# Moving a 2 MB weight load and two of its sums into the first pair of groups, and seeding a fourth output tile from the bias

## The chip, the cores and the metric

The kernel runs on one core of a Trainium2 chip. A core has five engines that run their own instruction queues side by side: PE (matrix products), DVE (vector), ACT (scalar and activations), POOL (GpSimd) and SP (here used to issue transfers). They meet only through semaphores. PE writes to PSUM, which is divided into banks; the other data lie in SBUF. Transfers between HBM and SBUF run on 16 DMA engines that all the queues share. The metric is the device time in microseconds (us); before the change it is 458.37 us, the median of three runs (458.12 to 458.46).

## What is computed

The input x has 32 sequences of 128 rows of 512 numbers. A conditioning vector per sequence gives a shift, a scale and a gate, once for each of two halves. In the reference, cut to what matters:

```
norm = layernorm(x) * (1 + scale) + shift;  norm = where(m, norm, 0)
ssm_out = where(m, mlp(norm, ssm) + mlp(norm, bwd), 0)
x = x + gate_msa * ssm_out                      # first half, masked rows only
ff_norm = layernorm(x) * (1 + scale_mlp) + shift_mlp
h = gelu(ff_norm @ ff_w1 + ff_b1)               # 512 -> 1024
return x + gate_mlp * (h @ ff_w2 + ff_b2)       # 1024 -> 512
```

`mlp(u, w)` is `gelu(u @ w1 + b1) @ w2 + b2`. All is float32.

## The kernel before

**First half.** Only the masked rows need it. They are gathered into four tiles of 128 rows, called slots. Their hidden layer is `hidden`, their second product is `project`. The output bias of the first half, `b2` (the sum of ssm_b2 and bwd_b2), is for tiles 0, 1 and 2 copied by ACT into a PSUM bank ahead of the products (`seeded_with_bias`, L236); the products then add to it. Tile 3 has no seed: its product goes into a bank of another pool, and DVE adds `b2` afterwards in `finish_late`, as the first of its three steps (L1367, L1369, L1370). The finished rows go to a buffer in HBM, `x1_rows`, from which POOL later gathers them back over the x tiles (`take_first_half`, L864). A row of `b2` is also kept in HBM (`b2_row`, L1346), for a loop at the end of the kernel that runs only where the masked rows fill more than the four tiles.

**Second half.** The 32 sequences are done in four pairs of two groups (four sequences to a group). Both products, `ff_w1` and `ff_w2` (here `fw1` and `fw2`), are done by a scheme with seven block products in place of eight, on two levels for the first. It needs differences of weight blocks. For `fw1`, DVE makes them in the opening; four of the larger ones (`weight_sums`) are stored to HBM (`t_rows`) and read back by `load_weights` into the two tiles `tw` when a stream needs them. For `fw2` there are four differences, `fw2_of.combine(0)` to `combine(3)` (line L387, 128x1024 numbers each): 0 gives t3, 1 replaces b12 of `fw2` in place, 2 gives t2 and 3 gives t4. Before the change 0 and 1 are made at the end of the opening, 2 and 3 inside the first pair's second product, which starts with the raw block b11, and then takes b12.

**FirstProduct** runs seven streams in the order 1, 2, 5, 6, 3, 7, 4. A stream has seven phases P1 to P7, of four matmuls each. From the third stream on a window weaves a new stream with the one before it: new P5, new P1, old P3, old P7, new P2, new P6, old P4 (positions 0 to 6). Window 2 starts stream 5, window 3 stream 6, window 4 stream 3, window 5 stream 7, window 6 stream 4. Streams 5 and 7 use one `tw` tile, 6 and 4 the other, so the third load waits for the last matmul of stream 5 and the fourth for that of stream 6. Between the phases stand:

- after P6 a DVE sum (L1121) that must be done before the same stream's P3;
- after P1 a seed, by DVE (L1140) or ACT (L1142), which must be done before P2;
- after P5 an ACT copy of the bank to SBUF (`p_m`, L1110), and additions on POOL (`with_p5`, L1147; `after`, L1176; `late_sum`, L1180), on which later L1121 and L1140 depend;
- ACT's copies and activations of the finished blocks (L1154, L1058).

The dictionary `fills` says what else is issued at a position: `put(3, 6, f)` issues f in window 3 after position 6.

**Order.** Nothing is scheduled by a planner in this part: every engine runs its instructions in the order in which the code issues them. On SP a transfer that has to wait holds everything behind it. In the opening SP issues, in this order: the transposing loads of xT, the 2 MB of `fw2` (`load_behind_gathers`, behind a one-element POOL memset), three stores of weight sums to `t_rows`, two stores to `x1_rows`, `b2_row`, `fb2`, two loads of the next pair's x, the last two stores to `x1_rows`, the first `tw` load, two more loads of x, the second `tw` load. PSUM tiles come from three pools that hand out their banks in turn; a new tile waits for the last reader of the bank it gets.

Of the kernel before, what the change touches and what calls it, by code (L numbers as in the profile page):

```python
# [14 lines left out]
ALU = mybir.AluOpType  # L15
# [7 lines left out]
def kernel(  # L23
# [49 lines left out]
    nc = tc.nc  # L73
# [23 lines left out]
    ps_h = ctx.enter_context(tc.tile_pool(name="ps_h", bufs=3, space=bass.MemoryType.PSUM))  # L97
# [16 lines left out]
    def broadcast_rows(t, vec, queue):  # L114

        n = vec.shape[0] // D
        each = t.shape[0] // n
        for j in range(n):
            queue.dma_start(
                t[j * each : (j + 1) * each, :],  # L120
                vec[ts(j, D)].rearrange("(o d) -> o d", o=1).to_broadcast([each, D]),
            )
# [12 lines left out]
    def load_blocks(t, w):  # L135
        nc.sync.dma_start(t, w.rearrange("(k p) f -> p k f", p=P))

    def load_behind_gathers(t, w):
        nc.gpsimd.memset(t[0:1, 0, 0:1], 0.0)
        load_blocks(t, w)  # L140
# [7 lines left out]
    w2 = ssm.tile([P, HC, D], F32, name="w2")  # L148
# [20 lines left out]
    def own_statistics(t, n, name):  # L169

        for i in range(n):
            st = stp.tile([P, 6], F32, tag="st", name=f"st_{name}_{i}")
            row = t[:, i]
            nc.vector.bn_stats(st, row[:, :D])
            nc.vector.bn_aggr(row[:, D : D + 2], st)
        var = t[:, :, D + 1]
        nc.vector.tensor_scalar(var, var, EPS, None, ALU.add)
        nc.gpsimd.tensor_tensor(var, var, half[:, :n], ALU.pow)

    def group_of_tiles(name):  # L180
        return xnp.tile([P, G, D], F32, tag="xn", name=f"xn_{name}")
# [19 lines left out]
    def hidden(xT, n, w, bcol, func, name, pool, parts=range(HC), after=None):  # L201

        h = []
        for f in parts:
            ph = ps_h.tile([P, 512], F32, tag="h", name=f"ph_{name}_{f}")
            for k in range(KC):
                nc.tensor.matmul(  # L207
                    ph[:, :n], w[:, k, ts(f, P)], xT[:, k, :], start=(k == 0), stop=(k == KC - 1)
                )
            t = pool.tile([P, n], F32, tag="h", name=f"h_{name}_{f}", bufs=HC)  # L210
            nc.scalar.activation(t, ph[:, :n], func, bias=biasT[:, bcol + f : bcol + f + 1])
            h.append(t)
            for g in (after or {}).get(f, ()):
                g()
        return h

    def project(i, h, w, name, between=None, bank=(ps_o, "o"), seeded=None):

        pool, tag = bank
        po = seeded or pool.tile([P, 512], F32, tag=tag, name=f"po_{name}_{i}")  # L220
        for f in range(HC):
            if between and f in between:
                between[f]()
            nc.tensor.matmul(  # L224
                po,
                h[f][:, ts(i, P)],
                w[:, f, :],
                start=(f == 0 and seeded is None),
                stop=(f == HC - 1),
                skip_group_check=seeded is not None,  # L230
            )
        return po

    def seeded_with_bias(at):
        po = ps_o.tile([P, 512], F32, tag="o", name=f"po_s{at}")
        nc.scalar.copy(po, b2)  # L236
        return po

    def gated(po, bias, gate, name):

        t = tp.tile([P, D], F32, tag="t", name=f"t_{name}")
        nc.vector.tensor_tensor(t, po, bias, ALU.add)
        nc.vector.tensor_tensor(t, t, gate, ALU.mult)
        return t
# [117 lines left out]
    def finish_slots(at, po, gate):  # L362
        t = tp.tile([P, 1, D + 2], F32, tag="t", name=f"t_s_{at}")
        row = t[:, 0, :D]
        nc.vector.tensor_tensor(row, po, gate, ALU.mult)
        nc.vector.tensor_tensor(row, row, xc[at], ALU.add)
        own_statistics(t, 1, f"s_{at}_x1")
        nc.sync.dma_start(x1_wide[ts(at, P), :], t[:, 0])
        return lambda: nc.sync.dma_start(x1_rows[ts(at, P), :], row)
# [20 lines left out]
    def load_side(p, side, spare=()):  # L390

        tiles = []
        for c in range(2):
            b = (2 * p + side) * G + 2 * c
            t = spare[c] if c < len(spare) else x_tile(b)
            nc.sync.dma_start(t, x[b : b + 2].rearrange("b s d -> s b d"))
            tiles.append(t)
        return tiles
# [184 lines left out]
    b2 = ssm.tile([P, D], F32, name="b2")  # L583
# [51 lines left out]
    fw2 = fwp.tile([P, HC, D], F32, name="fw2")  # L635
# [57 lines left out]
    def in_blocks(t):  # L693
        return t.rearrange("p g (h f) -> p (g h) f", f=2 * P)
# [22 lines left out]
    def store_weight_sums(*which, queue=nc.sync):  # L717
        for j in which:
            queue.dma_start(t_rows[j - 1, :, 4:], t_sum[j][1][:, :3])
            queue.dma_start(t_rows[j - 1, :, :4], t_sum[j][0])  # L720
# [30 lines left out]
    h1 = []  # L751
    for f in range(KC):
        hidden_of_tile(f, 1)
        for done in (f - 1, f) if f % 2 else ():
            t = ssm.tile([P, NH], F32, tag="h", name=f"h_s0_{done}", bufs=HC)
# [19 lines left out]
    po_s = [seeded_with_bias(0)]  # L775
# [4 lines left out]
    own_statistics(raw[2], 2, "x_2")  # L780
    b2_row = dram.tile([1, D], F32, name="b2_row")
    store_rows = [finish_slots(0, project(0, h1, w2, "s0", seeded=po_s[0]), gs[0])]
    own_statistics(raw[3], 2, "x_3")
    t = in_blocks(group_of_tiles("tw_3"))
    t_sum[3] = [t[:, :4], t[:, 4:]]
# [65 lines left out]
    of_x = {}  # L851
# [6 lines left out]
    fw2_of = Weights(fw2, HC // 2, D // 2, t_2)  # L858
# [69 lines left out]
    def turned(xn, xT, queues, which=range(4)):  # L928

        R = 32  # L930
        src = xn.rearrange("p k i (q c) -> p q k i c", c=R)
        dst = xT.rearrange("p k (i b c) -> p b k i c", b=P // R, c=R)
        for b in which:
            for q in range(P // R):
                queues[(b + q // 2) % len(queues)].dma_start(dst[ts(q, R), b], src[ts(b, R), q])  # L935
# [403 lines left out]
    def turn(k):  # L1339
        return lambda: transposed(1, xn_b, xT[1], k)  # L1340

    def turn_rows(b):
        return lambda: turned(xn, xT[0], (nc.sync, nc.scalar), (b,))

    def load_of_pair_1():
        nc.sync.dma_start(b2_row, b2[0:1, :])  # L1346
        broadcast_rows(fb2, ff_b2, nc.sync)
        x_of[1] = [load_side(1, 0, spare), None]

# [3 lines left out]
        3: [turn_rows(0), lambda: weight_sums(4)],  # L1353
        4: [turn_rows(1)],
        5: [turn_rows(2)],
        6: [turn_rows(3), lambda: load_behind_gathers(fw2, ff_w2), lambda: store_weight_sums(4, 1, 2)] + store_rows,
        7: [load_of_pair_1],
    }
    h1 = hidden(xT_t, NH, w1, 0, AF.Gelu, "s1", ssm, after=after)
# [1 line left out]
    for k in range(KC):  # L1361
        scaled(0, xT[0], k)

    def finish_late(at, po, bias=None):
        t = tp.tile([P, D], F32, tag="t", name=f"t_s_{at}")
        if bias is not None:
            nc.vector.tensor_tensor(t, po, bias, ALU.add)  # L1367
            po = t
        nc.vector.tensor_tensor(t, po, gs[at], ALU.mult)  # L1369
        nc.vector.tensor_tensor(t, t, xc[at], ALU.add)  # L1370
        nc.sync.dma_start(x1_rows[ts(at, P), :], t)

    finish_late(2, project(0, h1, w2, "s2", {2 * k: turn(k) for k in range(KC)}, seeded=po_s[2]))
    po = project(1, h1, w2, "s3", bank=(ps_h, "h"))
    of_x[0] = TokenBlocks(0, xT)
    for j in (1, 2):
        of_x[0].one(j)
    fw2_of.combine(0, 1)
    for j in (3, 4):
        of_x[0].one(j)  # L1380
    finish_late(3, po, b2)
    first_half.close()
    hp = straight.enter_context(tc.tile_pool(name="hp", bufs=1))
    gp = straight.enter_context(tc.tile_pool(name="gp", bufs=1))
# [25 lines left out]
    for p in range(NP):  # L1410
# [4 lines left out]
        def put(w, n, f, *args):  # L1415
            fills.setdefault(w, {}).setdefault(n, []).append(lambda: f(*args))
# [7 lines left out]
        for n, at in enumerate(((2, 4), (2, 4), (2, 6), (2, 6) if more_pairs else (3, 1))):  # L1424
            put(*at, now.token_sums, 4, n)
        put(3, 6, now.load_weights, 3)
        put(4, 6, now.load_weights, 4)
        second = SecondProduct(p, now.h, xs)
        if p == 0:
# [127 lines left out]
    with tc.If(more > 0):  # L1557
        b2 = lp.tile([P, D], F32, name="b2_l")
# [10 lines left out]
        with tc.For_i(0, more, 1):  # L1569
# [12 lines left out]
            for half_no, (mod, was, wbs, bias, bcol, func) in enumerate(  # L1582
# [25 lines left out]
                t = gated(project(0, h_l, wb, f"l{half_no}"), bias, gate_l, f"l{half_no}")  # L1608
# [59 lines left out]
```

## Time and profile before

The profiled execution took 457.94 us, of which the span of its instructions is 456.2 us. Over the span PE is busy 445.3 us (98%), DVE 332.8 (73%), ACT 176.9 (39%) and POOL 161.2 (35%). The granted clock of PE is 0.999 of full speed.

The table gives busy microseconds of each engine in stretches of the span, and the mean busy share of the 16 DMA engines. The opening ends, and the first pair's streams begin, at 84.45 us; the first pair's second product begins at 127.6, the second pair at 171.6.

| stretch, us | PE | DVE | ACT | POOL | DMA share |
|---|---|---|---|---|---|
| 60 to 70 | 10.00 | 8.58 | 2.37 | 6.02 | 0.63 |
| 70 to 80 | 10.00 | 7.56 | 7.53 | 0.00 | 0.97 |
| 80 to 90 | 9.80 | 9.70 | 2.50 | 0.00 | 1.00 |
| 90 to 100 | 7.26 | 8.05 | 3.59 | 6.45 | 1.02 |
| 100 to 110 | 10.00 | 8.77 | 5.19 | 8.45 | 0.15 |
| 110 to 130 | 20.00 | 14.04 | 10.42 | 16.25 | 0.27 |
| 130 to 150 | 20.00 | 18.83 | 7.47 | 5.76 | 0.58 |
| 150 to 180 | 30.00 | 20.96 | 14.28 | 0.00 | 0.49 |

A row is read against its length: PE is short of the stretch's length only where it waited. An engine can be far from full over a stretch and still be late for one instruction, so the waits of single instructions have to be read too. Where one line of the profile names what ended an idle time, it is the last of the awaited events.

### The profile page before, as it was taken

The page shows a single profiled execution, that of the slowest core. Times are in us where ns is not written, and L with a number is a line of the kernel's source. Part 1 is how long each engine was busy: PE and PEld are TensorE (multiplying, and loading weights), DVE is VectorE, ACT ScalarE, POOL GpSimd, SP SyncE. Part 2 cuts the span into 40 slices and gives each one's busy share as a digit, 9 for nine tenths or more (in the row PEclk, how much of TensorE's full clock was granted, in tenths as well). Part 3 has the DMA queues.
Part 4 walks back from the last instruction along what each step waited for, and adds up shares of the span by engine and source line. Part 5 has one row for each costly group of instructions (what it writes and reads, how often), then busy time and mean ns, then how long its engine had stood idle before and what let it go on. Part 6 is the DMA issues. An engine that isn't in the chain of part 4 may idle for free.

```text
span 456.2 us, 6196 instructions
## 1 busy us (share of the span) xinstructions
PE 445.3 (98%) x2161; PEld 370.9 (81%) x2161; DVE 332.8 (73%) x570; ACT 176.9 (39%) x387; POOL 161.2 (35%) x155
## 2 busy tenths in 40 slices
PE   8999999979999999999999999999999999999995
PEld 4784485668888888888888888888888888888884
DVE  4797887978779749895796398867963995534645
ACT  3123126244543551545435515454355154552000
POOL 4230560079770000697700006977000027560000
PEclk9999999999999999999999999999999999999999
DMA  7999549982208725822187258221772442222022
GB/s 233 382 352 403 232 70 261 339 343 96 80 22 221 115 60 203 290 96 82 34 214 106 64 198 293 94 84 43 201 111 62 152 149 82 80 92 94 0 93 96
DMA packets 83201, 70.98 MB, mean 156 GB/s; under 512 B 63292, under 2 KB 64268, under 8 KB 82142
## 3 DMA queue, kind: packets, MB, share of 16 engines
q1 hardware_dynamic: 67994, 58.41, 41.0%
q0 software_dynamic: 4400, 10.74, 7.0%
q10 hardware_dynamic: 10772, 1.39, 2.2%
q8 instruction: 19, 0.31, 0.3%
q14 instruction: 16, 0.13, 0.1%
HBM read 56.84 MB, written 13.70 MB: 155 GB/s over the span
## 4 chain that ended last, share of the span: by engine, by line
PE 80%; DMA 13%; DVE 4%; SPq 1%; issue 1%; POOL 0%; ACT 0%; POOLq 0%; ACTq 0%; DVEq 0%
PE a_o L1283 23%; PE a_m L1096 20%; PE e_o L1283 18%; PE e_m L1096 15%; DMA fw<-in_L_cond_ff_w_dram 7%; DMA tw<-t_rows 2%; DMA w<-in_L_cond_ssm_w_dram 1%; PE ph_s L207 1%; DVE t L387 1%; DMA xT<-xn 1%; DMA x_wide<-t_s 1%; PE last L1283 1%; SPq L935 1%; DMA x<-x_wide,slot_i 1%; DVE fw L387 0%
## 5 line engine op out<-in xcount | busy, mean ns | idle before, releaser
L1147 POOL TENSOR_TENSOR ha<-p_m,ha 128x512 f32<-128x512 f32 x20 | 25.8, 1289 | 176.8 <-ACT ha L1154 167.4
L1283 PE MATMUL e_o<-fw,ha 128*128 128x256 f32 x256 | 57.9, 379 | 0.0
L918 ACT ACTIVATE xT<-xT,modT 128x128 f32<-128x128 f32 x112 | 44.0, 480 | 33.0 <-DMA xT<-xn 32.1
L1283 PE MATMUL a_o<-t,hb 128*128 128x256 f32 x240 | 54.1, 379 | 0.0
L1283 PEld LDWEIGHTS e_o<-fw,ha 128*128 128x128 f32 x256 | 48.7, 190 | 6.5
L1283 PEld LDWEIGHTS a_o<-t,hb 128*128 128x128 f32 x240 | 45.7, 190 | 6.1
L1058 ACT ACTIVATE hb<-hb,biasT 128x256 f32<-128x256 f32 x64 | 29.0, 500 | 27.9 <-POOL hb L1180 19.4
L1110 ACT COPY p_m<-e_m 128x512 f32<-128x512 f32 x27 | 15.8, 585 | 50.1 <-PE e_m L1096 50.1
L864 POOL DMA_INDIRECT x<-x_rows,slot_i x24 | 28.5, 1186 | 6.8 <-issue 4.9
L224 PE MATMUL po_s<-w,h_s 128*128 128x512 f32 x64 | 28.7, 596 | 0.9 <-DMA w<-in_L_cond_bwd_w_dram 0.9
L1147 POOL TENSOR_TENSOR hb<-p_m,hb 128x512 f32<-128x512 f32 x20 | 29.4, 1470 | 0.3
L1283 PE MATMUL a_o<-t,s 128*128 128x256 f32 x128 | 28.9, 380 | 0.0
L1283 PE MATMUL a_o<-fw,ha 128*128 128x256 f32 x128 | 28.9, 379 | 0.0
L1283 PE MATMUL e_o<-fw,s 128*128 128x256 f32 x128 | 28.9, 379 | 0.0
L1154 ACT COPY ha<-e_m 128x512 f32<-128x512 f32 x32 | 18.5, 579 | 25.2 <-PE e_m L1096 24.7
L1283 PEld LDWEIGHTS a_o<-t,s 128*128 128x128 f32 x128 | 24.4, 190 | 3.2
L1283 PEld LDWEIGHTS a_o<-fw,ha 128*128 128x128 f32 x128 | 24.4, 190 | 3.3
L1283 PEld LDWEIGHTS e_o<-fw,s 128*128 128x128 f32 x128 | 24.4, 190 | 3.2
L1121 DVE TENSOR_TENSOR e_m<-a_m,ha 128x512 f32<-128x512 f32 x20 | 13.9, 697 | 16.7 <-POOL ha L1147 6.6
L1058 ACT ACTIVATE ha<-e_m,biasT 128x256 f32<-128x256 f32 x48 | 20.0, 467 | 14.7 <-PE e_m L1096 12.5
L1096 PE MATMUL a_m<-xT,tw 128*128 128x256 f32 x96 | 24.7, 380 | 0.0
L1126 DVE TENSOR_TENSOR hb<-a_m,hb 128x512 f32<-128x512 f32 x20 | 13.7, 685 | 15.0 <-PE a_m L1096 15.0
(235 smaller groups left out, 904.5 us busy)
## 6 DMA issues: line engine op xcount, KB each, us to landing
tw<-t_rows SPq DMA_DIRECT2D x16, 896.0 KB, 5.5
x<-in_x_dram SPq DMA_DIRECT2D x16, 512.0 KB, 12.0
gate<-gate_rows POOLq DMA_DIRECT2D x8, 1024.0 KB, 5.2
out_dram<-x SPq DMA_DIRECT2D x15, 512.0 KB, 4.4
xT<-xn SPq DMA_DIRECT2D x92, 64.0 KB, 2.4
fw<-in_L_cond_ff_w_dram SPq DMA_DIRECT2D x2, 2048.0 KB
ada_f<-in_L_cond_ffada_w_dram SPq DMA_DIRECT2D x4, 768.0 KB, 13.9
ada_a<-in_L_cond_ada_w_dram SPq DMA_DIRECT2D x4, 512.0 KB, 5.3
```

The lines of the kernel that those rows point to most:

```text
L207: nc.tensor.matmul(ph[:, :n], w[:, k, ts(f, P)], xT[:, k, :], start=(k == 0), stop=(k == KC - 1))
L224: nc.tensor.matmul(po, h[f][:, ts(i, P)], w[:, f, :], start=(f == 0 and seeded is None), stop=(f == HC - 1), skip_group_check=seeded is no ...
L864: nc.gpsimd.indirect_dma_start(out=xs[i // G][i % G // 2][:, i % 2], out_offset=None, in_=x1_rows, in_offset=bass.IndirectOffsetOnAxis(ap= ...
L918: nc.scalar.activation(out, src, AF.Identity, bias=shift, scale=scale)
L1058: nc.scalar.activation(dst[:, n], src[:, n], AF.Gelu_apprx_tanh, bias=biasT[:, f : f + 1])
L1096: nc.tensor.matmul(bank[:, ts(n, QT)], self.w_block(j, product)[:, ts(n, P)], self.x_block(j, product), start=(product in ("P1", "P5") and ...
L1110: nc.scalar.copy(p5, e)
L1121: nc.vector.tensor_tensor(e, a, p5, add)
L1126: nc.vector.tensor_tensor(dst, a, dst if prior else self.p5[j], add)
L1147: nc.gpsimd.tensor_tensor(self.place(RESULT[j], c), self.p5[j], other, ALU.add)
L1154: nc.scalar.copy(self.place(RESULT[j], c), src)
L1283: nc.tensor.matmul(part, src[:, k, ts(i, P)], w[product][:, k, :], start=(last and k == 0), stop=True, skip_group_check=True,)
```

## The change

It does three things.

1. `b2_row` is stored right after the first tile's rows, ahead of the third weight sums, and no longer ahead of the load of `fb2`.
2. A fourth bank is seeded with `b2` as soon as the first tile's bank has been read. Tile 3's product adds to it, and `finish_late` has two DVE steps instead of three.
3. The load of `fw2` leaves the opening, and the memset ahead of it goes. It is issued in the first pair at the end of window 3, between the third and the fourth `tw` load; `combine(0)` moves to the end of window 5 and `combine(1)` to position 3 of window 6. `combine(2)` and `combine(3)` stay.

```diff
     store_rows = [finish_slots(0, project(0, h1, w2, "s0", seeded=po_s[0]), gs[0])]
+    nc.sync.dma_start(b2_row, b2[0:1, :])
+    po_s.append(seeded_with_bias(3))
     own_statistics(raw[3], 2, "x_3")
...
     def load_of_pair_1():
-        nc.sync.dma_start(b2_row, b2[0:1, :])
         broadcast_rows(fb2, ff_b2, nc.sync)
...
-        6: [turn_rows(3), lambda: load_behind_gathers(fw2, ff_w2), lambda: store_weight_sums(4, 1, 2)] + store_rows,
+        6: [turn_rows(3), lambda: store_weight_sums(4, 1, 2)] + store_rows,
...
-    def finish_late(at, po, bias=None):
+    def finish_late(at, po):
         t = tp.tile([P, D], F32, tag="t", name=f"t_s_{at}")
-        if bias is not None:
-            nc.vector.tensor_tensor(t, po, bias, ALU.add)
-            po = t
         nc.vector.tensor_tensor(t, po, gs[at], ALU.mult)
...
-    po = project(1, h1, w2, "s3", bank=(ps_h, "h"))
+    po = project(1, h1, w2, "s3", seeded=po_s[3])
     of_x[0] = TokenBlocks(0, xT)
-    for j in (1, 2):
+    for j in range(1, 5):
         of_x[0].one(j)
-    fw2_of.combine(0, 1)
-    for j in (3, 4):
-        of_x[0].one(j)
-    finish_late(3, po, b2)
+    finish_late(3, po)
...
         put(3, 6, now.load_weights, 3)
+        if p == 0:
+            put(3, 6, load_blocks, fw2, ff_w2)
+            put(5, 6, fw2_of.combine, 0)
+            put(6, 3, fw2_of.combine, 1)
         put(4, 6, now.load_weights, 4)
```

## The prediction

> **What bounds the kernel.** I read the busy table first (PE 98% of the span), then busy time by stretch, then PE's timeline. From 51 us to the last matmul (448.03 + 3.47 = 451.5) PE is idle 0.39 us in 50 to 60, 0.20 in 80 to 90 and 2.74 in 90 to 100, and nowhere else; the other 4.7 us are the tail after it. So the kernel is bound by PE, and no edit behind 51 us can bring more than 3.3 us. PE's timeline names the two holes (start, duration, what ran, how often, idle before and what ended it):
>
> ```profile
> 88.77 1.03 PE L1096 MATMUL e_m<-s,fw 128*128 128x256 f32 x4
> 90.44 1.13 PE L1096 MATMUL e_m<-s,fw 128*128 128x256 f32 x4 [0.64 <-DVE e_m L1121]
> ...
> 94.00 1.03 PE L1096 MATMUL a_m_alone<-xT,t 128*128 128x256 f32 x4
> 97.33 1.10 PE L1096 MATMUL e_m<-sx,tw 128*128 128x256 f32 x4 [2.30 <-DMA tw<-t_rows]
> ```
>
> Groups of four start 0.864 us apart when nothing is late, so by starts the holes are 90.44 - 89.64 = 0.80 and 97.33 - 94.86 = 2.47.
>
> The first hole is DVE's and ACT's. These are their timelines:
>
> ```profile
> 81.69 1.23 DVE L387 TENSOR_TENSOR t<-fw 128x1024 f32<-128x1024 f32 x1
> 83.02 1.23 DVE L387 TENSOR_TENSOR fw<-fw 128x1024 f32<-128x1024 f32 x1
> ...
> 86.43 0.68 DVE L1367 TENSOR_TENSOR t_s<-po_s,b 128x512 f32<-128x512 f32 x1
> 87.15 0.69 DVE L1369 TENSOR_TENSOR t_s<-t_s,gs 128x512 f32<-128x512 f32 x1
> ...
> 88.01 0.58 ACT L1110 COPY p_m<-e_m_alone 128x512 f32<-128x512 f32 x1 [1.92 <-DVE t_s L1369]
> ```
>
> ACT's copy p_m takes memory that held gs, so it waits for L1369, behind both sums of the fw2 weights and the bias addition; the sum L1121 that PE wants comes after it.
>
> The second hole is the DMA's. In the chain of waits:
>
> ```profile
> 70.44 11.23 DMA fw<-in_L_cond_ff_w_dram
> ...
> 89.10 8.09 DMA tw<-t_rows
> ```
>
> The 2.1 MB of fw2 enter the queue ahead of the weight-sum stores; the load tw is issued at 89.10, after stores that those delay, and lands at 97.19. The DMA share is 0.92 to 1.08 throughout 70 to 100 us, bar one 2 us slice at 0.89.
>
> **The early edits.** The seed copy for the fourth tile is one ACT copy (row of the other seeds: 0.59 us). It needs the bank of the first tile, read until 44.85; ACT is idle from 38.5 to 51.17: nothing. The b2_row store (0.24 us on SP) now stands behind the store of 47.42 and ahead of one that is not ready until 50.60: nothing, and x_wide's second store at 55.42 is not reached. Later the stream-2 accumulator gets the fourth tile's bank, which L1369 frees: the tile ends at 84.6, L1369 at 85.4, PE wants it at 85.32: 0.1 us lost.
>
> **What goes.** DVE loses 2 x 1.23 (minus overlap, 2.4) and 0.68 us. Its four 1.22 us sums then end at 83.9, L1369 waits for PE and ends at 85.4 instead of 87.84, so p_m follows its matmuls at 87.3. What is late next is L1121 itself: its product ends at 89.05, plus 0.06 + 0.70 + 0.06 gives PE 89.87: the first hole shrinks by 0.57. Without 2.1 MB at the 0.41 MB/us of the slices 80 to 86, the stores land 5 us earlier; SP then waits for the last x1 store (DVE ends its row at 86.05) and issues tw at 86.5. Landing takes 4.6 to 5.5 us in the groups of this kernel: 92.0, where PE now comes at 94.27. The second hole closes: 97.33 becomes 94.27, **3.1 us** gained there.
>
> **What is late next.** PE's lead then meets two engines that were only just in time. DVE: it runs without idle from 101.13 to 111; before that it idled 1.69 us for PE. Its L1121 of stream 5 can move 2.2 us, and had 0.55 to spare; L1140 of stream 6 2.2 and 0.2: PE keeps **2.4**. POOL is tighter:
>
> ```profile
> 92.28 1.27 POOL L1147 TENSOR_TENSOR ha<-p_m,ha 128x512 f32<-128x512 f32 x1 [25.34 <-ACT ha L1154]
> 93.51 1.71 POOL L1147 TENSOR_TENSOR hb<-p_m,hb 128x512 f32<-128x512 f32 x1
> 95.88 1.11 POOL L864 DMA_INDIRECT x<-x_rows,slot_i x1 [0.66 <-DMA tw<-t_rows]
> ...
> 107.95 1.28 POOL L1147 TENSOR_TENSOR ha<-p_m,ha 128x512 f32<-128x512 f32 x1
> ...
> 110.40 1.27 POOL L1176 TENSOR_TENSOR ha<-ha 128x512 f32<-128x512 f32 x1
> ...
> 111.71 0.70 DVE L1140 TENSOR_TENSOR e_m<-a_m,ha 128x512 f32<-128x512 f32 x1 [0.57 <-POOL ha L1176]
> ```
>
> Eight gathers (12.05 us) and five additions run back to back. They start 0.57 earlier (PE's first hole) and lose about 0.36 of the 0.66 wait (0.30 stays between gathers): 0.93. L1140 ended at 112.41 and PE used it at 112.94, 0.47 spare after 0.06 of signal. So PE keeps 0.93 + 0.47 = **1.4 us**; the other 1.7 come back as stalls near 108 and 110 us.
>
> **The moved load.** On SP fw2 now stands behind the third tw load (109.68 before, about 107 now) and ahead of the fourth (due one window, 6 us, later). 0.92 + 2.1 MB at 0.41 is 7.4 us: fw2 is there by about 116, its first sum is due at 121.3. The third tw, ahead in the queue, lands in about 4.6 us, near 111.5, wanted at 114.1. The fourth is issued near 114.3, lands near 119 behind the rest of fw2, wanted at 120.2. Nothing from the load; cover 2.6, 1.2 and 5 us. If fw2 shared its bandwidth evenly with the third tw, both would land near 115.5: 1.4 us lost.
>
> **The moved sums.** Two DVE sums of 1.23 us go into windows 5 and 6, about 122.8 and 125.9 by the old clock. DVE has 0.63 + 0.67 + 1.03 + 1.36 us of idle there, and L1140 behind the first is then ready at 124.67 for PE's 125.03. By durations alone they cost nothing. Against this stands a rule of the Trainium skill (SBUF — State Buffer, "Who interferes with whom"): a DVE instruction with two SBUF inputs and a GpSimd one that reads SBUF exclude each other, the first to start holding on. At 81.69 POOL was idle; here it adds. The rows:
>
> ```profile
> 118.14 1.38 DVE L1416 TENSOR_TENSOR fb_step<-fb 128x256 f32<-128x256 f32 x1
> ...
> 126.41 1.30 POOL L1180 TENSOR_TENSOR ha<-ha 128x512 f32<-128x512 f32 x1 [2.54 <-ACT ha L1154]
> ```
>
> L1416, beside POOL's addition of 117.97, took 1.38 us where this shape takes 0.42 (L1025's shortest), so the lock is in this trace. The second sum (125.91 to 127.13) would hold POOL's 126.41 for 0.72. POOL then runs back to back to 134.71, where ACT waits for it and then seeds a_o (136.27 to 136.86) for PE at 137.11: 0.2 spare, **0.5 lost**. Bounds: 0, if POOL finds gaps; 1.2 if the block sum behind (L1230) has to alternate with POOL too. The first sum meets only POOL's 4-element root (L902): 0, at most 0.7. DVE's four later sums of this kind meet no POOL work.
>
> **Sum.** -1.4 + 0.5 = -0.9: the profiled 457.94 (span 456.2 and 1.74 around it) becomes 457.0, and the median of the runs shown, 458.37, which is 0.43 above, becomes **457.5 us**. Pairs 2 to 4 keep their PE spacing.
>
> **Rivals.**
> A, more of the hole is kept: the gathers run at their shortest (0.99 us against a mean of 1.24: 2 us earlier), POOL no longer decides, DVE caps at 2.4, sums free or 0.5: 456.0 to 456.5. For: the DMA is calmer. Against: the gathers' 0.30 us gaps and lengths show no DMA wait. Chance 0.27.
> B, the case above, 1.4 minus 0 to 1.2: 457.0 to 458.2. Chance 0.56.
> C, slower: the lock at windows 5 and 6. Both sums and the L1230 blocks alternate with POOL: 0.7 + 1.6 lost, and once the moved sums lose over 1.4 us the change is a loss; with tw's 1.4 as well it would be 2 us. Time 459.3. For: L1416's row; against: DVE's idle time there. Chance 0.14.
> D, the tw wait does not go: the chain names ACT's L1154, which ended at 89.09, as what released the load. If that were its real need, tw would be issued near 88.5, land by 93.1 to 94.0, and still be in time; 457.5 to 458.2. Chance 0.03; the built order gives it no such work, only buffers' old readers.
>
> Within 0.2% is 0.92 us, about what a measurement of this kernel tells from no change. B lies on that edge: half of it is faster. Faster 0.27 + 0.28 = 0.55; same 0.31; slower 0.14. The range, 455.9 to 459.0, takes in A's better end and most of C.
>
> **What would show it.** Right: no wait of PE on tw; p_m near 87.3; new PE waits on L1121 and L1140 near 108 to 110, ended by POOL; fw2 landing before 118; POOL's addition near 125 delayed behind a 1.23 us sum and a short PE wait before a_o near 135.5. Wrong: a PE wait on tw at 114 or 120, a DVE wait on fw2, or a fully kept 3 us.

## The result and the profile after

The changed kernel takes 459.28 us, the median of 20 runs (458.00 to 460.92); the kernel before, run beside it, takes 458.25 (20 runs, 456.88 to 461.75). The ratio is 1.0016 with a 95% interval of 1.0000 to 1.0031, or 0.7 us more; the two medians are 1.03 us apart. In this comparison the change costs 0.7 to 1.0 us, about the 0.92 us (0.2%) that the prediction took for the edge of no change, and on the slow side. Forecast were 457.5 us and a range of 455.9 to 459.0, so the median is missed by 1.8 us and lies 0.3 us above the range.

The profiled execution took 459.17 us, with a span of 457.4. Its busy table:

```profile
PE 447.2 (98%) x2161; PEld 369.7 (81%) x2161; DVE 333.0 (73%) x569; ACT 177.6 (39%) x388; POOL 163.3 (36%) x154
```

PE is still the bound. POOL is busy 2.1 us longer (161.2 before) with one instruction fewer; three of its instructions, shown further down, take 1.9 us of that (2.11, 1.84 and 1.60 us in place of 1.03, 1.30 and 1.28). PE's timeline for the first pair (start, duration, what ran, how often, in brackets the idle time before it and what ended it) answers to the two holes shown of before:

```profile
94.49 1.03 PE L1098 MATMUL a_m_alone<-xT,t 128*128 128x256 f32 x4
95.36 1.03 PE L1098 MATMUL e_m<-sx,tw 128*128 128x256 f32 x4
...
112.49 1.13 PE L1098 MATMUL e_m<-xT,fw 128*128 128x256 f32 x4 [0.45 <-DVE e_m L1142]
...
120.36 1.03 PE L1098 MATMUL a_m<-xT,t 128*128 128x256 f32 x4
122.03 1.10 PE L1098 MATMUL e_m<-s,tw 128*128 128x256 f32 x4 [0.64 <-DMA tw<-t_rows]
...
138.30 1.99 PE L1285 MATMUL a_o<-fw,ha 128*128 128x256 f32 x8 [0.49 <-ACT a_o L1224]
```

The wait of 2.30 us on the first `tw` is gone: 95.36 follows 94.49 by 0.87, the full pace. In its place stand three waits that the kernel before did not have: one for a sum that POOL feeds (112.49), one for the fourth `tw` load (122.03), and one for a seed of a_o (138.30). (Lines of the file after the change have numbers 2 higher here.) That the first of the three hangs on POOL is seen one engine further back, in POOL's timeline (its last gather and two of the additions behind it) and in DVE's:

```profile
106.95 1.00 POOL L866 DMA_INDIRECT x<-x_rows,slot_i  x1 [0.31 <-issue]
107.98 1.28 POOL L1149 TENSOR_TENSOR ha<-p_m,ha 128x512 f32<-128x512 f32 x1
...
110.44 1.26 POOL L1178 TENSOR_TENSOR ha<-ha 128x512 f32<-128x512 f32 x1
```

```profile
111.73 0.70 DVE L1142 TENSOR_TENSOR e_m<-a_m,ha 128x512 f32<-128x512 f32 x1 [0.93 <-POOL ha L1178]
```

To set kernels against each other I count from the first matmul of the first stream, `t0`, since the opening alone moves `t0` between 84.45 and 85.97 us in the fourteen profiles of this study, with no order by kernel: PE's matrix products of the opening already start 0.9 us later in the profile of after at 35 us, where nothing has been changed yet. "End" is the span less `t0`. The other columns are the starts of: stream 5 (P5, where the first `tw` is needed), P2 of stream 3, P5 of stream 4 (the fourth `tw`), the second product, its second and third blocks (here "block 2" and "block 3", the latter needs a_o's seed), and the second pair.

| kernel | t0 | P5 of 5 | P2 of 3 | P5 of 4 | product 2 | block 2 | block 3 | pair 2 | end |
|---|---|---|---|---|---|---|---|---|---|
| before | 84.45 | 12.88 | 28.49 | 37.12 | 43.17 | 48.35 | 52.66 | 87.20 | 371.75 |
| after | 85.34 | 10.02 | 27.15 | 36.69 | 42.81 | 47.98 | 52.96 | 87.59 | 372.06 |

After is 2.86 us ahead at stream 5, 1.34 at P2 of stream 3, 0.43 at P5 of stream 4, and 0.30 behind at block 3. So the gain was made, and was given back within the same pair, on three stretches. On the first of them the 0.45 us at 112.49 are only the last and largest of several short stalls: from stream 5 to P2 of stream 3 PE takes 17.13 us, where it took 15.61 before.

### The profile page after: what moved, and what is told of

The parts are those of the page before. It is cut to its first block, busy times and chain, and to the rows that moved or that the text cites. A ratio compares the mean times of both kernels' runs of the same rounds, so it can differ in the third digit from the quotient of the medians.

```text
span 457.4 us, 6190 instructions
## 1 busy us (share of the span) xinstructions
PE 447.2 (98%) x2161; PEld 369.7 (81%) x2161; DVE 333.0 (73%) x569; ACT 177.6 (39%) x388; POOL 163.3 (36%) x154
## 4 chain that ended last, share of the span: by engine, by line
PE 80%; DMA 8%; POOL 5%; issue 2%; DVE 1%; ACT 1%; SPq 1%; POOLq 0%; DVEq 0%
PE a_o L1285 23%; PE e_o L1285 17%; PE a_m L1098 16%; PE e_m L1098 13%; PE po_s L224 5%; DMA w<-in_L_cond_bwd_w_dram 5%; PE ph_s L207 3%; POOL x L866 2%; DMA tw<-t_rows 1%; DMA x<-in_x_dram 1%; DMA xc<-in_x_dram,token_i_s 1%; PE last L1285 1%; SPq L136 1%; POOL ha L1149 1%; PE pm_f L303 1%
## 5 line engine op out<-in xcount | busy, mean ns | idle before, releaser
L1098 PE MATMUL e_m<-s,fw 128*128 128x256 f32 x92 | 23.8, 381 | 0.0
```

What stands on the lines that cost most here:

```text
L1098: nc.tensor.matmul(bank[:, ts(n, QT)], self.w_block(j, product)[:, ts(n, P)], self.x_block(j, product), start=(product in ("P1", "P5") and ...
```

## The experiments

Two parts of the change alone come first, then each new wait taken out by itself, then combinations, and last the two kernels again.

**The seed and the early `b2_row` store alone** (`fw2` and its sums as in the kernel before):

```diff
-        6: [turn_rows(3), lambda: store_weight_sums(4, 1, 2)] + store_rows,
+        6: [turn_rows(3), lambda: load_behind_gathers(fw2, ff_w2), lambda: store_weight_sums(4, 1, 2)] + store_rows,
...
-    for j in range(1, 5):
+    for j in (1, 2):
+        of_x[0].one(j)
+    fw2_of.combine(0, 1)
+    for j in (3, 4):
         of_x[0].one(j)
...
-            put(3, 6, load_blocks, fw2, ff_w2)
-            put(5, 6, fw2_of.combine, 0)
-            put(6, 3, fw2_of.combine, 1)
```

> Parts 1 and 2 of the change alone: b2_row stored early and the fourth tile seeded; fw2 and its two sums stay in the opening. Counted from the first stream's first matmul to the end of the span (371.75 us before, 372.06 after). Theory (the gain and its losses all come from the moved load and sums): PE's first hole shrinks by up to 0.6 us, the wait on tw swallows it, because tw still lands behind fw2; 371.5 to 371.8, ratio to before 0.999 to 1.000. Rival (the seed and the store make the opening later by the 0.9 us that the two profiles differ by at the first stream): first stream at 85.3 and ratio 1.002.

Measured: 459.22 against 457.93 us, ratio 1.0031 (1.0020 to 1.0042), end 372.68. This is slower and a miss. PE's timeline of this kernel, and DVE's:

```profile
87.21 1.10 PE L1098 MATMUL a_m<-xT,fw 128*128 128x256 f32 x4 [1.66 <-DVE t_s L1367]
...
113.30 1.13 PE L1098 MATMUL e_m<-xT,fw 128*128 128x256 f32 x4 [0.44 <-DVE e_m L1142]
```

```profile
81.64 1.22 DVE L387 TENSOR_TENSOR t<-fw 128x1024 f32<-128x1024 f32 x1
82.96 1.23 DVE L387 TENSOR_TENSOR fw<-fw 128x1024 f32<-128x1024 f32 x1
...
86.38 0.68 DVE L1367 TENSOR_TENSOR t_s<-po_s,gs 128x512 f32<-128x512 f32 x1
```

With the fourth seed, tile 3's bank is the one that the second stream needs next. It is freed by L1367, and in this kernel the two `fw2` sums stand ahead of L1367 on DVE. So the seed is only cheap together with the removal of those sums; I had priced the seed at 0.1 us in the whole change and had not seen that the sums' going is what keeps it small.

**The `fw2` move alone** (no fourth seed, `b2_row` where it was):

```diff
-    po = project(1, h1, w2, "s3", seeded=po_s[3])
+    po = project(1, h1, w2, "s3", bank=(ps_h, "h"))
...
-    finish_late(3, po)
+    finish_late(3, po, b2)
```

> Part 3 alone: fw2 loaded in window 3 and its sums made in windows 5 and 6; the fourth tile has no seed and b2_row is stored late. Theory: the same picture as the whole change, no wait on the first tw, then stalls near 110 (POOL), 122 (tw behind fw2) and 138 (POOL behind the moved sum); 371.9 to 372.3 us from the first stream on. Rival (seed and early store are needed for the gain, since the buffer of tw waits for the b2_row store): PE waits on tw at 95 by over 1 us, 373 us or more.

Measured: 458.74 against 457.93 us, ratio 1.0009 (0.9994 to 1.0023), end 371.90, P5 of stream 5 at 9.76. The same three waits are there: 0.44 (the POOL-fed sum), 0.56 (`tw`) and 0.48 us (a_o). So the move of `fw2` makes the whole picture. The seed and the early store, which the two kernels differ by, cost 0.26 us at the second stream (10.02 - 9.76) and bring nothing.

**The load earlier**, right behind the second `tw` load, the sums as in after:

```diff
     now.load_weights(2)
+    load_blocks(fw2, ff_w2)
...
-            put(3, 6, load_blocks, fw2, ff_w2)
```

> The changed kernel, with the load of fw2 issued right behind the second tw load (about 89 us) instead of behind the third. Theory: the fourth tw load landed 6.5 us after its issue only because fw2 stood ahead of it; here it lands in 4.6 to 5.5 us, the wait near 122 goes and 0.8 us are won: 371.2 to 371.4 us from the first stream on, ratio to before 0.998 to 1.000. Rival (the load itself is late because SP reaches it late, 115.38): the wait stays at 0.6 us and the time is that of the change. A cost that could show: gathers or the second tw slowed by fw2, a wait on tw near 102.

Measured: 458.11 against 457.93 us, ratio 1.0000 (0.9984 to 1.0015), end 371.30, P2 of stream 3 at 27.13, P5 of stream 4 at 35.87. SP issues `fw2` at 88.99 in place of 108.76. The distance between those two steps falls from 9.54 to 8.74 us (8.63 in before), and PE's list of waits has no `tw` in it. So the load's place behind the third `tw` costs 0.8 us.

**The second sum earlier**, from position 3 of window 6 to position 1, the load as in after:

```diff
-            put(6, 3, fw2_of.combine, 1)
+            put(6, 1, fw2_of.combine, 1)
```

> The changed kernel, with the second fw2 sum two positions earlier (window 6, position 1), where POOL was idle from 124.98 to 126.94. Theory (DVE's two-input sum and POOL's addition exclude each other): POOL's L1182 starts unhindered and takes 1.27 us in place of 1.84, the block sum L1232 takes 0.68 in place of 1.76, and PE's wait of 0.49 us on ACT's seed a_o near 138 goes: 371.3 to 371.5 us from the first stream on. Rival (POOL is late there because of its backlog of gathers, whatever DVE does): L1182 and the wait on a_o stay.

Measured: 457.84 against 457.93 us, ratio 0.9997 (0.9986 to 1.0008), end 371.36. The wait for a_o is gone: from block 2 to block 3 it is 4.32 us, where after has 4.98 and before 4.31. The wait on the fourth `tw` stays (0.32 us). First the timeline of DVE in after, then that of POOL in after, then POOL's in this kernel:

```profile
122.86 1.22 DVE L387 TENSOR_TENSOR t<-fw 128x1024 f32<-128x1024 f32 x1
...
126.44 1.22 DVE L387 TENSOR_TENSOR fw<-fw 128x1024 f32<-128x1024 f32 x1
127.57 1.76 DVE L1232 TENSOR_TENSOR s<-hb 128x512 f32<-128x512 f32 x1
```

```profile
122.87 2.11 POOL L904 TENSOR_TENSOR rstd<-ve,half 128x4 f32<-128x4 f32 x1
126.94 1.84 POOL L1182 TENSOR_TENSOR ha<-ha 128x512 f32<-128x512 f32 x1 [1.96 <-ACT ha L1156]
128.85 1.60 POOL L1149 TENSOR_TENSOR ha<-p_m,ha 128x512 f32<-128x512 f32 x1
```

```profile
126.41 1.51 POOL L1182 TENSOR_TENSOR ha<-ha 128x512 f32<-128x512 f32 x1 [1.65 <-ACT ha L1156]
128.00 1.26 POOL L1149 TENSOR_TENSOR ha<-p_m,ha 128x512 f32<-128x512 f32 x1
```

In after, POOL's addition of 126.94 runs 1.84 us beside the sum of 126.44, and then DVE's block sum L1232 and POOL's next addition hold each other up (1.76 and 1.60). The ends show them taking turns: the sum ends at 127.66, the addition 1.12 us later, L1232 0.55 us after that, the next addition another 1.12 us on. With the sum in the gap before, POOL takes 1.51 and 1.26. The first sum stretches POOL's four-element root L904 from 1.04 us (in the kernel with the seed alone) to 2.11, and PE never waits for it.

**Both of these edits together:**

> The changed kernel with both repairs: fw2 loaded behind the second tw load, and the second sum at window 6, position 1. Theory: both losses behind the gathers go, the lead of 1.35 us that the first pair has at P2 of stream 3 (28.49 us after the first stream's start before the change, 27.13 to 27.15 after) is kept to the end: 370.3 to 370.6 us from the first stream's start to the end of the span (371.75 before), ratio 0.996 to 0.998. Rival (a further wait stands behind the two, so that repairs do not add): 370.9 or more.

Measured: 457.78 against 458.27 us, ratio 0.9987 (0.9972 to 1.0001), end 370.86. PE has one wait left, 0.45 us before P2 of stream 3. The end is 0.3 us later than I had written: the three stretches from P2 of stream 3 to block 3 are each 0.11 to 0.14 us longer than in before, and the block sum L1232 still takes 1.73 us.

**Both, and the last of the eight gathers moved** behind position 4 of window 5, out of POOL's row of gathers:

```diff
-    take_first_half(1, x_of[1])
+    take_first_half(1, x_of[1], range(2 * G - 1))
...
+            put(5, 4, take_first_half, 1, x_of[1], (2 * G - 1,))
```

> As the one with both repairs, and the eighth gather of the first pair (POOL, 1.3 us with its gap) moved behind POOL's additions for stream 7, window 5 position 4. Theory (POOL's row of eight gathers and five additions limits the lead to 1.35 us): P2 of stream 3 comes 0.9 to 1.2 us earlier, at 26.0 to 26.3 us after the first stream's start, where DVE's chain becomes the limit; the whole from there on 369.2 to 369.7 us, ratio 0.994 to 0.996. Rival (DVE's L1142 and L1123 set the pace there and only look as if POOL ended their waits): P2 at 27.1, no gain.

Measured: 456.96 against 458.27 us, ratio 0.9971 (0.9954 to 0.9988), end 369.94. P2 of stream 3 starts at 26.28, 0.86 us earlier than in after, and the wait there is gone. So POOL's row of gathers was the cap. The end is again later than expected, by 0.2 us, the size of a wait for a_o (0.24) that comes up behind it.

**The same gather moved in after, nothing else:**

> The changed kernel with only the eighth gather moved; the load and the sums stay where the change has them. Theory (the losses are in series and the fourth tw load is tied to the transfer of fw2, not to PE): P2 of stream 3 at 26.0 to 26.3 us as in the kernel with both repairs, but the fourth tw lands hardly earlier, PE's wait there grows from 0.64 to about 1.4 us, and the end is 371.6 to 372.0 us from the first stream's start. Rival (each loss is a fixed price): 371.0 us.

Measured: 458.33 against 458.27 us, ratio 0.9992 (0.9976 to 1.0009), end 371.43. By the landmarks PE is 0.87 us earlier than in after at P2 of stream 3 (26.28), and it keeps 0.74 of that at P5 of stream 4 (35.95) and at block 3 (52.22). PE's timeline of this kernel:

```profile
120.92 1.10 PE L1098 MATMUL e_m<-s,tw 128*128 128x256 f32 x4 [0.88 <-DMA tw<-t_rows]
...
137.19 3.07 PE L1285 MATMUL a_o<-fw,ha 128*128 128x256 f32 x13 [0.49 <-ACT a_o L1224]
```

The wait on `tw` grows from 0.64 to 0.88 and not to the 1.4 of the theory: SP reaches the fourth load earlier too (114.03 in place of 115.38, of which 0.37 are the earlier `t0`), and the landing takes 6.75 us, 0.24 more. So the transfer of `fw2` does not hold the fourth load where it was. The end lies between what theory and rival expected, but the rival has the mechanism: each loss is close to a fixed price. Against the end of after (372.06), the load alone brings 0.76 us, the sum alone 0.70 and the gather alone 0.63; all three together bring 2.12, and their sum is 2.09.

**The best of these without the fourth seed** (both edits, the gather moved, tile 3 and `b2_row` as in before):

> Both repairs and the moved gather, but without parts 1 and 2 of the change: the fourth tile has no seed, DVE adds b2, and b2_row is stored late. Theory (once the sums of fw2 have left the opening, the seed brings nothing, and its bank costs PE 0.15 us at P1 of stream 2): within 0.3 us of the kernel with seed, 369.0 to 369.7 us from the first stream's start. Rival (the seed and the early store carry part of the gain): 370.2 us or more.

Measured: 456.61 against 458.27 us, ratio 0.9952 (0.9935 to 0.9969), end 369.76, a little above what was expected. This version beats both kernels: by medians it is 1.7 us under the kernel before, and 2.7 under the 459.28 of the changed one, which was measured in another set of runs. From the version with the seed it is not clearly apart: the two intervals overlap, and the ends differ by 0.18 us.

**The two kernels again**, for the size of the difference:

> The kernel before, unchanged, run as if it were a change: what two sets of runs of the same program differ by, and a second profile of its opening. Theory (the first stream starts anywhere from 84.4 to 85.5 us by the arrival of the early loads, whatever the change): ratio 1 within 0.2%, 371.6 to 371.9 us from the first stream on, a start that differs from 84.45 by up to 1 us. Rival (the kernels without fw2 in the opening start later): a start of 84.3 to 84.6 again.

> The changed kernel once more. Theory: the same three waits (near 112, 122 and 138 us), 371.9 to 372.2 us from the first stream on, ratio to before 1.0005 to 1.002. Rival (the 1.0016 of its first runs was chance and hides a small gain): below 1.0.

Measured: 458.31 and 459.14 us beside 458.28 of the kernel before, ratios 1.0004 (0.9985 to 1.0024) and 1.0005 (0.9992 to 1.0018), so that this second comparison alone does not tell after from before. The second profile of after repeats its first (P2 of stream 3 at 27.15, end 372.18). That of before does not repeat: its wait on `tw` is 1.59 us in place of 2.30, its `t0` 85.97 and its end 371.23, both outside what was expected. Two more profiles of the kernel before were taken for that:

> The kernel before, unchanged, to see how large its wait on tw is from one execution to the next. Two profiles of it had 2.30 and 1.59 us there, and from the streams' first matmul to P2 of the third stream 28.49 and 27.64 us, while the changed kernel had 27.15 in both of its profiles. Theory: in the kernel before, this distance is set by when the first tw load lands behind the rest of the opening's transfers, so it scatters (27.4 to 28.6 here), and from there to the end of the first pair's first product nothing scatters: P2 of the third stream to P5 of the fourth 8.63, and P5U to P1V 4.31, within 0.05. Rival: the 2.30 of the first profile is the rule, and 1.59 an accident of a late opening: 28.4 to 28.6 whenever the first matmul comes before 85 us.

> The kernel before, unchanged, once more, for the same question. Theory: first matmul of the streams to P2 of the third stream between 27.4 and 28.6 us, differing from the other profiles by over 0.2; P2 of the third to P5 of the fourth 8.63 and P5U to P1V 4.31, within 0.05. Rival: 28.4 to 28.6 whenever the first matmul comes before 85 us.

Measured, one execution each (granted clock 0.997 and 0.998): P2 of stream 3 at 27.50 and 27.08, ends 371.27 and 370.40. From the chain of waits, one line of each of these three executions (again, third, fourth), and from PE's timeline the group that waits:

```profile
90.49 7.37 DMA tw<-t_rows
```

```profile
98.00 1.10 PE L1096 MATMUL e_m<-sx,tw 128*128 128x256 f32 x4 [1.59 <-DMA tw<-t_rows]
```

```profile
89.75 7.23 DMA tw<-t_rows
```

```profile
97.11 1.10 PE L1096 MATMUL e_m<-sx,tw 128*128 128x256 f32 x4 [1.44 <-DMA tw<-t_rows]
```

```profile
89.42 6.81 DMA tw<-t_rows
```

```profile
96.37 1.10 PE L1096 MATMUL e_m<-sx,tw 128*128 128x256 f32 x4 [1.03 <-DMA tw<-t_rows]
```

The load took 8.09, 7.37, 7.23 and 6.81 us in the four profiles, and PE's wait is this less 5.78 or 5.79 in every one of them. The rival, that 2.30 us is the rule where `t0` is early, falls: `t0` was 84.90 in the fourth. The theory's range was 27.4 to 28.6, and the fourth profile (27.08) lies below it; that the distance scatters with the load's landing holds, and the distances behind it are as it said (8.63 and 8.64; 4.31 and 4.32).

## Why the prediction was wrong

The kernel before is therefore better told by the mean of its four profiles, and after by that of its two. The distances add up as follows (microseconds, after less before, from the landmarks):

| stretch | before | after | difference | predicted |
|---|---|---|---|---|
| t0 to P2 of stream 3 | 27.68 (28.49, 27.64, 27.50, 27.08) | 27.15 (27.15, 27.15) | -0.53 | -1.4 |
| to P5 of stream 4 | 8.63 | 9.60 (9.54, 9.65) | +0.96 | 0 |
| to block 2 | 11.23 | 11.29 | +0.06 | 0 |
| to block 3 | 4.31 | 4.98 | +0.67 | +0.5 |
| to pair 2 | 34.54 | 34.63 | +0.09 | 0 |
| pair 2 to the end | 284.78 (284.55 to 285.06) | 284.47 | -0.31 | 0 |
| sum | 371.16 | 372.12 | +0.96 | -0.9 |

The sum of +0.96 fits the medians (1.03 and 0.86 us apart in the two comparisons); the ratios, 1.0016 and 1.0005, make it 0.7 and 0.2 us. The prediction's sum was off by 1.9 us, and two rows make 1.8 of it.

**The step that failed: "The moved load ... Nothing from the load; cover 2.6, 1.2 and 5 us."** The fourth `tw` was to land near 119 behind the rest of `fw2`, 1.2 us before it is wanted. SP's timeline of after:

```profile
88.87 19.83 SPq L1044 DMA_DIRECT2D tw<-t_rows  x2
108.76 0.55 SPq L136 DMA_DIRECT2D fw<-in_L_cond_ff_w_dram  x1
115.38 0.32 SPq L1044 DMA_DIRECT2D tw<-t_rows  x1
```

and its chain of waits:

```profile
115.38 6.51 DMA tw<-t_rows
```

The issue came as I had it (114.3, and 0.9 for the later `t0`); the landing did not: 6.51 us after the issue, where I had taken about 4.7. It is the wait on `tw` near 120 that the prediction named as a sign of being wrong. The load lands at 121.89, and PE's group in front began at 120.36, so it was due at 121.22. The windows of after (stretch; its length; then busy microseconds of PE, its weight loads, DVE, ACT and POOL; granted clock, DMA share, GB/s) show what was moved meanwhile:

```profile
108.00:110.00 2.00, 2.00 (x10) 1.47 (x8) 1.10 (x4) 1.17 (x2) 2.00 (x2) 1.00 0.39 85
110.00:112.00 2.00, 2.00 (x9) 1.44 (x8) 1.03 (x3) 0.59 (x1) 2.00 (x3) 1.00 0.94 326
112.00:114.00 2.00, 1.55 (x8) 1.36 (x8) 1.81 (x4) 0.34 (x1) 2.00 (x2) 1.00 0.90 269
114.00:116.00 2.00, 2.00 (x11) 1.77 (x10) 0.59 (x1) 0.50 (x2) 2.00 (x3) 1.00 1.02 343
```

I had priced the 3.8 MB of two `tw` and `fw2` at the 410 GB/s of the opening's slices 80 to 86. These first slices moved 269 to 343; only the two from 116 to 120 reached 406 and 424. Over 110 to 116 that is 1.88 MB in place of 2.46, and the missing 0.58 MB are 1.4 of the 1.8 us; the other 0.4 are not accounted for. A cover of 1.2 us was smaller than the doubt in a rate read in another stage. In the kernel before, the four slices from 70 to 78, where its own load of `fw2` began beside other transfers, had moved 134, 231, 341 and 306 GB/s. The kernel with the load behind the second `tw` shows that it is `fw2` in front of the fourth load: it takes away 0.80 of the 0.91 us, and the wait with it. Why those slices moved less, at a DMA share of 0.90 to 1.02, no run shows.

**The step that was mis-sized: "The second hole closes: 97.33 becomes 94.27, 3.1 us gained there", kept as 1.4.** That the hole closes is right, and so is the cap: POOL's eight gathers hold P2 of stream 3, as the prediction worked out, and against the one profile I had, the lead there is 1.34 us (1.4 predicted). But the lead is counted from a hole of 2.30 us, which is the deepest of four. In after this stretch is set by POOL and repeats to 0.01 us; in before it is set by when a transfer lands and ranges over 1.4 us. The mean gain is 0.53, and against the fourth profile there is none (27.08 and 27.15). With a median 0.4 us above that profile I should have asked whether the hole belongs to it; no view of a single execution could tell.

**The moved sums.** The lock was chosen as the likelier course at 0.5 us; measured 0.67. A GpSimd addition and a DVE sum of two SBUF operands exclude each other here, as the Trainium skill has it (SBUF — State Buffer, "Who interferes with whom"): the addition takes 1.84 us beside the sum and 1.27 without (in the kernel with the seed alone). So these two engines meet here without a semaphore. By durations alone it would have been nothing. The upper bound's mechanism, alternation with the block sum behind, was there too: L1232 took 1.76 us, where the others take 0.68. The run with the sum in the gap shows this whole 0.67 to be the sum's place: it returns to 4.32.

**The early edits.** "0.1 us lost" for the bank was 0.26 by the pair of runs with and without both early edits. No wait of PE is ended by the early store or the seed copy.

**The rivals.** A, the hole kept further, was refuted as a forecast but its size comes true once one gather is moved: 26.28, 2.21 us before the first profile's 28.49, near DVE's cap of 2.4. C gave the sign and the sort of outcome, but that its 459.3 meets the 459.28 is luck: the lock lost 0.67 of the 2.3 us that C asked for, the load, priced at nothing in the forecast, lost 0.96, and the lead that both eat into was 0.53 and not 1.4. D is out: the wait on `tw` went.

What stays open: why the first `tw` of the kernel before takes 6.8 to 8.1 us from one execution to the next, so that the -0.53 rests on four profiles that differ by up to 1.4 us; why the slices at 110 to 116 moved less; and the -0.31 us behind the second pair, which is no larger than the spread of its own row (284.55 to 285.06).

## What to carry to other kernels

A wait that ends with a transfer has no size until several executions have been profiled: here it was 1.0 to 2.3 us, and the one profile at hand had the largest. When a large load is moved in front of a small one on the same queue, price the small one's landing behind all the bytes at the lowest rate that the trace shows while such a load runs, and ask for more cover than the difference between that and the highest. And a gain on the bound engine is only a lead: list what was just in time behind it (here POOL's gathers, the next load, a seed) and move these as well, or the lead turns into waits; moving one gather, one load and one sum turned a ratio of 1.0016 into 0.9971, and 0.9952 without the seed.

## What the runs showed of the hardware

- A transfer of 0.9 MB took 6.81 to 8.09 us in four executions of one kernel, 6.51 behind 2 MB on its queue in another.
- A POOL operation of 128x4 numbers, 1.04 us alone, took 2.11 us when it began 0.01 us after a DVE sum of two SBUF operands. Its size did not protect it: it was held for 1.07 of the sum's 1.22 us.
- A POOL addition and two DVE sums of two SBUF operands each, issued close together, ran in turn: 1.84 and 1.60 us for two additions that take 1.27 elsewhere, 1.76 us for a sum that takes 0.68.
- The first matmul of the streams came between 84.45 and 85.97 us in fourteen profiles. The distances between the landmarks of the first pair agree to 0.01 us in the profiles of one kernel wherever no transfer sets the pace, so a difference of 0.1 us can be read from them, while the ratio of two sets of 20 runs still has an interval of 0.7 us to either side. Behind the second pair's start the distance to the end differs by up to 0.5 us in four profiles of one kernel.
